# First attention of a hybrid block: outputs kept by channel and divided by GpSimd, maxima turned by VectorE

## The chip, the core and the metric

The kernel runs on one core of a Trainium2 chip. The metric is the device time of one execution in microseconds (us), here the median of three runs. A profile holds one execution. In it PE is TensorE (the matrix engine), PEld its weight loads, DVE VectorE, ACT ScalarE, POOL GpSimd, and SPq the queue of SyncE, which issues nearly all DMAs of this kernel. Each engine works through its own list of instructions in order, and engines wait for each other by semaphores.

## What is computed

A block of four layers on x of 1024 tokens x 512 channels, all in fp32: attention A (32 heads of 16 channels, causal, rotary), a mixture-of-experts layer, attention B (32 heads of 128 channels), and the same mixture again. The change concerns attention A alone:

```python
xq, xk = rotary(x @ wq.T), rotary(x @ wk.T)          # 32 heads of 16
scores = einsum("bqhd,bkhd->bhqk", xq, xk) * hd**-0.5
scores = where(causal, scores, -1e30)
probs  = softmax(scores)                              # max, exp, divide by the sum
out    = einsum("bhqk,bkhd->bqhd", probs, xv).reshape(B, T, C)
x      = x + out @ wo.T
```

## The kernel before

Attention A takes its heads in eight groups of four (index c, 0 to 7). A head has 16 channels and is padded to 32 partitions, so four heads fill 128. Channel 16 of a head in `qT` holds the negated row maximum, and in `kT` it is 1: one matmul then gives score minus maximum. Column 16 of `v_p` is 1, so that row 16 of an output is the sum of the exponentials.

Two passes run side by side, one group apart. The row pass of group c+1 (`row_scores`, L325) makes scores with queries on partitions, and VectorE takes their maxima (`maxima`: L342 for a first part, L345 for the rest). `with_maxima` turns the maxima from partitions to a row and puts them into `qT`. The column pass of group c (`col_scores`, L378) makes the scores again with keys on partitions, ScalarE takes exp (L397), and `product` (L417) multiplies with the values into one PSUM bank `outs[c, qc]`, for each half qc of the queries. When that is complete, ScalarE copies it (L426), and `normalize` divides.

`step(rc, cc, n)` is one of nine pieces of both passes, done in two half steps of two heads each. A half step has scores for two row tiles and two column tiles, then the maxima, the exponentials, what is due in the list `later`, and half of a product that is two pieces behind. `later` holds functions with a count of how many calls of `due` they wait. All score tiles, and everything else that goes through PSUM here, rotate through the seven banks of the pool `ps_s`; a tile has to be read by VectorE or ScalarE before its bank is written again. The output bank `ps_o` is a single one. For c below 7, the outputs of qc=1 are complete in piece 8 of their own group and those of qc=0 in piece 1 of the next group.

The order on each engine is made by a scheduler from the order of the program, so an instruction may stand ahead of where the program calls it; TensorE's order around the change is scores, half a product, scores, half a product.

In `normalize` (L430) TensorE turns the output back to tokens on partitions (four transposes, tile `tp_o`), ScalarE copies it (L437), VectorE inverts the sums (L439) and GpSimd multiplies (L441). `tail` and `projected` then turn every token tile again to channels on partitions (`gather`: four transposes, tile `tp_ao`, and a copy by VectorE, L1043) and multiply with `wo` (`out_projection`, L1049). The first two token tiles are done right after the attention, the other six inside the loop of the first mixture layer, each with a layer norm, its transposes (`tp_f`) and the router's matmuls (`pr_f`, L568).

Of the kernel before, what the change touches and what calls it, by code (L numbers as in the profile page):

```python
# [9 lines left out]
F32 = mybir.dt.float32  # L10
BF16 = mybir.dt.bfloat16
AF = mybir.ActivationFunctionType
ALU = mybir.AluOpType
# [3 lines left out]
P = 128  # L17
T = 1024
NT = T // P
C = 512  # L20
# [44 lines left out]
class Block:  # L65
# [174 lines left out]
    def attend_a(self, ctx_pool, pt, work, ps_s, ps_o, qT, kT, v_p, project_qk, project_v, midway, tail):  # L240
        nc, tc = self.nc, self.tc
        HC = P // PADA
        with ExitStack() as ctx:
            cp = ctx.enter_context(tc.tile_pool(name="a_c", bufs=1))
            qk = ctx.enter_context(tc.tile_pool(name="a_qk", bufs=2))
            o_sb = []

            next(project_qk)

# [44 lines left out]
            def neg(c, half):  # L294

                if (c, half) not in negs:
                    negs[c, half] = qk.tile([P, HC, NT // 2], F32, tag="neg", name=f"neg{c}_{half}", bufs=3)
                return negs[c, half]
# [56 lines left out]

            def with_maxima(c, half):

                rows = HC * NT // 2
                ps = ps_s.tile([P, QC], F32, tag="s", name=f"tp_m{c}{half}")[:rows, :P]
                nc.tensor.transpose(ps, neg(c, half).rearrange("p h i -> p (h i)"), self.ident)  # L360
                t = qk.tile([P, P], F32, tag="negT", name=f"negT{c}_{half}")[:rows, :]
                nc.scalar.copy(t, ps)
                for j in range(HC):
                    row = j * PADA + DA
                    nc.sync.dma_start(
                        qT[row : row + 1, c, half * QC : (half + 1) * QC].rearrange("o (i t) -> o i t", t=P),
                        t[j * NT // 2 : (j + 1) * NT // 2, :],
                    )

            def col_scores(c, n, heads, made):  # L370

# [27 lines left out]
            def product(c, n, p):  # L399

                pieces = col_pieces(c, n)
                middle = pieces[-1][-1] // 2
                steps = by_cols(c)
                for lo, hi in ((0, middle), (middle, 2 * middle)):
                    for qc, b, x0, _, at, end in pieces:
                        p0, p1 = max(lo, at), min(hi, end)
                        if p0 >= p1:
                            continue
                        first = (c, qc) not in outs
                        if first:  # L410
                            outs[c, qc] = ps_o.tile([P, QC], F32, tag="o", name=f"oT{c}_{qc}")
                        last = p1 == end and b == [x[1] for y in steps for x in y if x[0] == qc][-1] and all(
                            x[0] != qc for y in steps[n + 1 :] for x in y
                        )
                        o = outs[c, qc]
                        for j in range(HC):
                            nc.tensor.matmul(  # L417
                                o[rows_of(j), x0 + p0 - at : x0 + p1 - at],
                                lhsT=v_cols(b, c * HC + j),
                                rhs=p[:, j, p0:p1],  # L420
                                start=first,
                                stop=last,
                            )
                        if last:
                            oT = work.tile([P, QC], F32, tag="w", name=f"oTs{c}_{qc}")
                            nc.scalar.copy(oT, o)  # L426
                            later.append([0, lambda qc=qc, oT=oT: normalize(c, qc, oT)])
                    yield

            def normalize(c, qc, oT):  # L430
                if not o_sb:
                    o = ctx_pool.tile([P, NT, C], F32, tag="o", name="o")
                    o_sb.extend(o[:, i] for i in range(NT))
                ps = self.transpose4(ps_s, [oT[:, i * P : (i + 1) * P] for i in range(4)], f"o{c}{qc}", tag="s")
                pv = ps.rearrange("p a (h d) -> p a h d", d=PADA)
                os = qk.tile([P, 4, HC, DA + 1], F32, tag="os", name=f"os{c}_{qc}")
                nc.scalar.copy(os, pv[:, :, :, : DA + 1])  # L437
                rs = qk.tile([P, 4, HC], F32, tag="rs", name=f"rsa{c}_{qc}")
                nc.vector.reciprocal(rs, os[:, :, :, DA])  # L439
                for a in range(4):  # L440
                    nc.gpsimd.tensor_tensor(  # L441
                        o_sb[qc * 4 + a][:, c * HC * DA : (c + 1) * HC * DA].rearrange("p (h d) -> p h d", d=DA),
                        os[:, a, :, :DA],
                        rs[:, a, :].unsqueeze(2).to_broadcast([P, HC, DA]),
                        ALU.mult,
                    )

            def drain(gens):
                gens = list(gens)
# [10 lines left out]
            def due():  # L460

                for x in list(later):
                    x[0] -= 1
                    if x[0] < 0:
                        later.remove(x)
                        x[1]()

            def step(rc, cc, n):
# [8 lines left out]
                for half in range(2 if both else 1):  # L477
# [11 lines left out]
                    if cc is not None:  # L489
                        exponentials(cc, n, cols, madeT, p)  # L490
                    due()
                    next(turns, None)
                drain([turns])
                if rc is not None:

                    for half in range(2):
                        if n == max(m for m, y in enumerate(by_rows(rc)) for x in y if x[0] // 4 == half):
                            later.append([0, lambda half=half: with_maxima(rc, half)])


            for i in range(1, NT):
# [13 lines left out]
            for item in pending:  # L515
                due()
                drain([product(*item)])
            tail(o_sb, ps_s, work, later)
        return o_sb

# [490 lines left out]
def hybrid_block_kernel(  # L1013
# [23 lines left out]
    ao = ctx.enter_context(tc.tile_pool(name="a_out", bufs=1))  # L1037
    wo = ao.tile([P, KC, C], F32, tag="wo", name="a_wo")

    def gather(o, i, work, tp, wtag, tag):  # L1040
        ps = blk.transpose4(tp, [o[i][:, k * P : (k + 1) * P] for k in range(KC)], f"ao{i}", tag)
        oT = work.tile([P, KC * P], F32, tag=wtag, name=f"aoT{i}").rearrange("p (k t) -> p k t", t=P)
        nc.vector.tensor_copy(oT, ps)  # L1043
        return oT

    def out_projection(i, oT, ps_m, tag):
        pm = ps_m.tile([P, C], F32, tag=tag, name=f"pm_ao{i}")
        for kc in range(KC):
            nc.tensor.matmul(pm, lhsT=oT[:, kc, :], rhs=wo[:, kc, :], start=(kc == 0), stop=(kc == KC - 1))  # L1049
        nc.vector.tensor_add(blk.x[i], blk.x[i], pm)  # L1050

    def tail(o, ps, work, later):
        oTs = [gather(o, i, work, ps, "w", "s") for i in range(2)]
        out_projection(0, oTs[0], ps, "s")
        while later:
            later.pop(0)[1]()
        out_projection(1, oTs[1], ps, "s")

    weights = [w_baseT, w_rhT, lora_B, b_base]
    f_ctx = ExitStack()  # L1060
# [8 lines left out]
    def projected(work, tp, ps_m):  # L1069
        yield  # L1070
        yield
        oT = gather(o, 2, work, tp, "oT", "tp")
        for i in range(2, NT):
            nxt = gather(o, i + 1, work, tp, "oT", "tp") if i + 1 < NT else None
            out_projection(i, oT, ps_m, "pm")
            oT = nxt
            yield

    xnT, xn = [], []
# [85 lines left out]
```

## Time and profile before

| | us |
|---|---|
| median of 3 runs | 1640.02 (1639.93 to 1641.65) |
| the profiled execution | 1641.65 |
| its span, first to last instruction | 1639.6 |
| TensorE busy in it | 1621.2 |
| VectorE, ScalarE, GpSimd busy | 1099.2, 551.5, 350.8 |
| from the first column scores to the end of the last product of attention A | 119.95 to 387.1 |
| from there to the end of the last output projection | 387.1 to 428.0 |

Busy time is a share of the span by engine. Groups of instructions are listed by line, engine, operation and tile with their mean duration; a line of the timeline has start, duration, engine, line, operation, the tiles written and read, and in square brackets the idle time before it and what ended it. Transposes by TensorE all have line L99, so they are told apart by their tiles.

### The profile page before, as it was taken

Reading aid. Unit: us, or ns where it says so; the run is one execution under the profiler, and the core shown is the slowest. Engines: PE = TensorE matmul, PEld = TensorE weight load, DVE = VectorE, ACT = ScalarE, POOL = GpSimd, SP = SyncE. Lnnn points to the kernel's source line nnn. Section 1 sums busy time; section 2 is a strip of 40 time slices with the busy share of each in tenths; the row PEclk is TensorE's granted clock in tenths of the full one; section 3 lists DMA queues with packets and bytes.
Section 4 is the critical chain, followed back from the end, with each engine's and each line's share of the span. In section 5 each row is a group of like instructions: output and inputs, shape, how many; then the busy total and the mean of one; then the engine's idle time right before and its main releaser. Section 6 shows DMA issues by size and latency. Waiting matters only on the chain.

```text
span 1639.6 us, 32629 instructions
## 1 busy us (share of the span) xinstructions
PE 1621.2 (99%) x13320; PEld 955.1 (58%) x13320; DVE 1099.2 (67%) x2832; ACT 551.5 (34%) x1202; POOL 350.8 (21%) x524
## 2 busy tenths in 40 slices
PE   9999999999999999999999999999999999999989
PEld 5545555555565667566655665756665566556654
DVE  4557777762635876867777677676767767777762
ACT  2316565664222332233233223223323322322230
POOL 3000000002222323123223212222322221221140
PEclk9999999999999999999999999999999999999999
DMA  5000000001012201200200210120020011000001
GB/s 199 1 1 2 2 2 3 2 3 40 1 53 66 62 2 43 49 27 26 65 27 26 47 46 1 40 52 27 27 65 27 27 43 56 1 27 27 2 1 51
DMA packets 60870, 52.08 MB, mean 32 GB/s; under 512 B 5745, under 2 KB 47473, under 8 KB 60721
## 3 DMA queue, kind: packets, MB, share of 16 engines
q1 hardware_dynamic: 59408, 46.06, 9.8%
q0 software_dynamic: 784, 2.90, 0.5%
q8 instruction: 104, 1.70, 0.4%
q10 hardware_dynamic: 528, 1.05, 0.2%
q14 instruction: 46, 0.37, 0.1%
HBM read 30.98 MB, written 2.10 MB: 20 GB/s over the span
## 4 chain that ended last, share of the span: by engine, by line
PE 73%; DVE 3%; POOL 1%; ACT 1%; issue 0%; ACTq 0%; DVEq 0%
PE s L825 15%; PE pq L779 14%; PE o L869 13%; PE wo L676 13%; PE kv L734 7%; PE pm_f L633 3%; PE or L869 3%; PE pm_ao L1049 1%; PE st L805 1%; PE pm_f L634 1%; PE tp_k L99 0%; DVE p L827 0%; PE pr_f L568 0%; PE oT L417 0%; POOL x L559 0%; DVE pT L852 0%
## 5 line engine op out<-in xcount | busy, mean ns | idle before, releaser
L834 ACT ACTIVATE p<-p,nm 128x1024 f32<-128x1024 f32 (+7 forms) x256 | 198.1, 774 | 405.8 <-DVE nm L832 363.3
L837 POOL TENSOR_SCALAR p<-p,rs 128x1024 f32<-128x1024 f32 (+7 forms) x256 | 190.3, 745 | 645.7 <-DVE rs L836 621.8
L825 PE MATMUL s<-kT,qT 128*128 128x512 f32 (+3 forms) x768 | 296.0, 493 | 1.9 <-DVE p L827 1.8
L852 DVE STREAM_TRANSPOSE pT<-p 128x640 f32<-128x640 f32 (+4 forms) x256 | 169.0, 670 | 127.5 <-PE o L869 83.8
L779 PE MATMUL pq<-xnTb,wq 128*128 128x512 f32 x512 | 243.0, 597 | 0.0
L676 PE MATMUL wo<-wo,oT 128*128 128x512 f32 x512 | 240.7, 593 | 1.8 <-DVE nm L832 1.8
L827 DVE SCALAR_TENSOR_TENSOR p<-s,rq,rel 128x512 f32<-128x512 f32 (+3 forms) x384 | 224.0, 601 | 24.6 <-PE s L825 23.4
L825 PEld LDWEIGHTS s<-kT,qT 128*128 128x128 f32 x768 | 140.8, 190 | 164.8 <-issue 117.2
L869 PEld LDWEIGHTS o<-pT,va 32*128 32x128 f32 x5248 | 210.7, 185 | 25.5 <-issue 17.9
L869 PE MATMUL o<-pT,va 32*128 32x256 f32 (+5 forms) x5248 | 220.0, 321 | 0.0
L831 DVE TENSOR_REDUCE nm<-p 128x1 f32<-128x1024 f32 (+7 forms) x256 | 188.8, 738 | 2.9
L397 ACT ACTIVATE p<-sT 128x512 f32<-128x512 f32 (+1 forms) x292 | 155.7, 592 | 97.7 <-PE s L325 46.2
L325 PE MATMUL s<-kT,qT 32*128 32x512 f32 (+3 forms) x768 | 164.1, 520 | 0.0
L378 PE MATMUL sT<-qT,kT 32*128 32x128 f32 (+3 forms) x1152 | 155.4, 401 | 0.2 <-DMA qT<-negT 0.2
L676 PEld LDWEIGHTS wo<-wo,oT 128*128 128x128 f32 x512 | 94.6, 190 | 89.0 <-issue 76.3
L779 PEld LDWEIGHTS pq<-xnTb,wq 128*128 128x128 f32 x512 | 92.4, 190 | 88.8 <-issue 79.7
L734 PE MATMUL kv<-wkv,xnTb 128*128 128x256 f32 x512 | 116.5, 380 | 0.8 <-DVE qT L789 0.5
L378 PEld LDWEIGHTS sT<-qT,kT 32*128 32x128 f32 x1152 | 80.9, 184 | 50.8 <-issue 24.6
L734 PEld LDWEIGHTS kv<-wkv,xnTb 128*128 128x128 f32 x512 | 96.2, 190 | 20.0 <-issue 4.0
L342 DVE TENSOR_REDUCE part<-s 128x1 f32<-128x512 f32 x128 | 81.9, 686 | 36.3 <-PE s L325 32.3
L417 PE MATMUL oT<-p,v_p 128*32 128x128 f32 (+1 forms) x1552 | 89.8, 332 | 0.0
L441 POOL TENSOR_TENSOR o<-os,rsa 128x64 f32<-128x64 f32 x64 | 16.7, 292 | 323.5 <-DVE rsa L439 308.5
(154 smaller groups left out, 1617.6 us busy)
## 6 DMA issues: line engine op xcount, KB each, us to landing
va<-v SPq DMA_DIRECT2D x256, 64.0 KB
wq<-in_b_WqT_dram SPq DMA_DIRECT2D x8, 1024.0 KB
wo<-in_b_WoT_dram SPq DMA_DIRECT2D x8, 1024.0 KB
x<-in_x_dram SPq DMA_DIRECT2D x8, 256.0 KB
wkv<-in_b_WkT_dram SPq DMA_DIRECT2D x8, 256.0 KB
wkv<-in_b_WvT_dram SPq DMA_DIRECT2D x8, 256.0 KB
out_dram<-x SPq DMA_DIRECT2D x8, 256.0 KB
wq<-in_a_wqT_dram ACTq DMA_DIRECT2D x1, 1024.0 KB
```

Source lines behind the costliest of these rows:

```text
L325: nc.tensor.matmul(made[j][:, at:end], lhsT=qT[rows_of(j), c, i * P : (i + 1) * P], rhs=kT[rows_of(j), c, kc * QC : kc * QC + end - at], s ...
L378: nc.tensor.matmul(made[j][:, at:end], lhsT=kT[rows_of(j), c, b * P : (b + 1) * P], rhs=qT[rows_of(j), c, qc * QC + x0 : qc * QC + x1], st ...
L676: nc.tensor.matmul(ps, lhsT=oTs[g, h][:, t * P : (t + 1) * P], rhs=wo[:, h, :], start=(h == heads[0]), stop=(h == heads[-1]))
L734: nc.tensor.matmul(ps.rearrange("p a b -> p (a b)"), lhsT=xnT[:, kc, i * P : (i + 1) * P], rhs=wkv[:, kc].rearrange("p a b -> p (a b)"), s ...
L779: nc.tensor.matmul(ps, lhsT=wq[:, kc, hh * DB : (hh + 1) * DB], rhs=xnT[:, kc, cols], start=(kc == 0), stop=(kc == KC - 1))
L825: nc.tensor.matmul(s, lhsT=qT[:, i * P : (i + 1) * P], rhs=kT[:, lo:hi], start=True, stop=True)
L827: nc.vector.scalar_tensor_tensor(p[:, lo:hi], s, rq[:, i : i + 1], rel[:, at + lo : at + hi], ALU.mult, ALU.add)
L831: nc.vector.tensor_reduce(nm, p[:, :w], AX.X, ALU.max, negate=True)
L834: nc.scalar.activation(p[:, :w], p[:, :w], AF.Exp, bias=nm, scale=slope, accum_out=ss)
L837: nc.gpsimd.tensor_scalar(p[:, :w], p[:, :w], rs, 1.0, ALU.mult, ALU.mult)
L852: nc.vector.transpose(PT[:, i : i + (NT - 1) * (m - 1) + 1 : NT - 1, :], p[:, : m * P].rearrange("p (j k) -> p j k", k=P))
L869: nc.tensor.matmul(cols(o[:, a], j), lhsT=vs[g][rows, j * NB + b, :], rhs=moving(j, rows, slice(b * B, (b + 1) * B)), start=(j == js[0] an ...
```

## The change

Outputs of attention A stay with channels on partitions. `normalize` is called as soon as the output bank is copied. It issues five DMAs: one that spreads the four rows of sums over 128 partitions of 16 numbers (`sums`), and four that put each head's 16 channels into the tile that the output projection will read (`to`). Two functions go into `later`: `invert` (VectorE inverts the sums; one DMA brings them back to four rows of `over`, and another spreads each of these over 16 partitions) and `multiply` (GpSimd multiplies 64 partitions x 512 in place). The transposes of `normalize` and `gather` and the copies behind them are gone, and the output projections read `outs_sb` directly.

`with_maxima` is called at the end of the step, not one `due` later. VectorE turns the 128x16 maxima in 32x32 blocks, the 16 columns written twice to fill a block; four DMAs then write, each one block of 32 query positions of all four heads, 16 pieces of 128 bytes. Before, TensorE and ScalarE made the turn and there was one DMA per head, four pieces of 512 bytes.

Where a step has only one of the two passes, `due` is called twice.

```diff
             def with_maxima(c, half):
-                rows = HC * NT // 2
-                ps = ps_s.tile([P, QC], F32, tag="s", name=f"tp_m{c}{half}")[:rows, :P]
-                nc.tensor.transpose(ps, neg(c, half).rearrange("p h i -> p (h i)"), self.ident)
-                t = qk.tile([P, P], F32, tag="negT", name=f"negT{c}_{half}")[:rows, :]
-                nc.scalar.copy(t, ps)
-                for j in range(HC):
-                    row = j * PADA + DA
-                    nc.sync.dma_start(
-                        qT[row : row + 1, c, half * QC : (half + 1) * QC].rearrange("o (i t) -> o i t", t=P),
-                        t[j * NT // 2 : (j + 1) * NT // 2, :],
-                    )
+                t = qk.tile([P, B], F32, tag="negT", name=f"negT{c}_{half}")
+                twice = neg(c, half).rearrange("p h i -> p (h i)").unsqueeze(1).to_broadcast([P, 2, B // 2])
+                nc.vector.transpose(t.rearrange("p (a m) -> p a m", a=2), twice)
+                to = qT[:, c, half * QC : (half + 1) * QC].rearrange("(j r) (i a t) -> j r a i t", r=PADA, a=P // B, t=B)
+                for a in range(P // B):
+                    m = a * B
+                    nc.sync.dma_start(to[:, DA, a], t[m : m + B // 2, :])
...
                         if last:
-                            oT = work.tile([P, QC], F32, tag="w", name=f"oTs{c}_{qc}")
+                            oT = qk.tile([P, QC], F32, tag="oT", name=f"oTs{c}_{qc}")
                             nc.scalar.copy(oT, o)
-                            later.append([0, lambda qc=qc, oT=oT: normalize(c, qc, oT)])
+                            normalize(c, qc, oT)
...
             def normalize(c, qc, oT):
-                if not o_sb:
-                    o = ctx_pool.tile([P, NT, C], F32, tag="o", name="o")
-                    o_sb.extend(o[:, i] for i in range(NT))
-                ps = self.transpose4(ps_s, [oT[:, i * P : (i + 1) * P] for i in range(4)], f"o{c}{qc}", tag="s")
-                pv = ps.rearrange("p a (h d) -> p a h d", d=PADA)
-                os = qk.tile([P, 4, HC, DA + 1], F32, tag="os", name=f"os{c}_{qc}")
-                nc.scalar.copy(os, pv[:, :, :, : DA + 1])
-                rs = qk.tile([P, 4, HC], F32, tag="rs", name=f"rsa{c}_{qc}")
-                nc.vector.reciprocal(rs, os[:, :, :, DA])
-                for a in range(4):
-                    nc.gpsimd.tensor_tensor(
-                        o_sb[qc * 4 + a][:, c * HC * DA : (c + 1) * HC * DA].rearrange("p (h d) -> p h d", d=DA),
-                        os[:, a, :, :DA],
-                        rs[:, a, :].unsqueeze(2).to_broadcast([P, HC, DA]),
-                        ALU.mult,
-                    )
+                if not outs_sb:
+                    outs_sb.append(ctx_pool.tile([P, KC, T], F32, tag="o", name="o"))
+                at = c % 2 * HC * DA
+                to = outs_sb[0][at : at + HC * DA, c // 2, qc * QC : (qc + 1) * QC]
+                sums = qk.tile([P, QC // B], F32, tag="sums", name=f"sums{c}_{qc}")
+                over = qk.tile([P, QC], F32, tag="over", name=f"over{c}_{qc}")
+                row = P // 2 - at
+                by_head = oT.rearrange("(j r) t -> j r t", r=PADA)
+                nc.sync.dma_start(sums, by_head[:, DA, :].rearrange("j (x e) -> j x e", x=B))
+                for j in range(HC):
+                    nc.sync.dma_start(to[j * DA : (j + 1) * DA, :], by_head[j, :DA, :])
+                def invert():
+                    nc.vector.reciprocal(sums, sums)
+                    inverses = over[row : row + HC, :]
+                    nc.sync.dma_start(inverses.rearrange("j (x e) -> j x e", x=B), sums)
+                    nc.sync.dma_start(over[at : at + HC * DA, :], inverses.unsqueeze(1).to_broadcast([HC, DA, QC]))
+                def multiply():
+                    nc.gpsimd.tensor_tensor(to, to, over[at : at + HC * DA, :], ALU.mult)
+                later.append([3, invert])
+                later.append([8, multiply])
...
                     due()
+                    if not both:
+                        due()
...
-                            later.append([0, lambda half=half: with_maxima(rc, half)])
+                            with_maxima(rc, half)
...
-    def gather(o, i, work, tp, wtag, tag):
-        ps = blk.transpose4(tp, [o[i][:, k * P : (k + 1) * P] for k in range(KC)], f"ao{i}", tag)
-        oT = work.tile([P, KC * P], F32, tag=wtag, name=f"aoT{i}").rearrange("p (k t) -> p k t", t=P)
-        nc.vector.tensor_copy(oT, ps)
-        return oT
-
-    def out_projection(i, oT, ps_m, tag):
+    def out_projection(oT, i, ps_m, tag):
...
-            nc.tensor.matmul(pm, lhsT=oT[:, kc, :], rhs=wo[:, kc, :], start=(kc == 0), stop=(kc == KC - 1))
+            nc.tensor.matmul(pm, lhsT=oT[:, kc, i * P : (i + 1) * P], rhs=wo[:, kc, :], start=(kc == 0), stop=(kc == KC - 1))
...
-    def tail(o, ps, work, later):
-        oTs = [gather(o, i, work, ps, "w", "s") for i in range(2)]
-        out_projection(0, oTs[0], ps, "s")
+    def tail(oT, ps, later):
+        out_projection(oT, 0, ps, "s")
         while later:
             later.pop(0)[1]()
-        out_projection(1, oTs[1], ps, "s")
+        out_projection(oT, 1, ps, "s")
...
     def projected(work, tp, ps_m):
         yield
         yield
-        oT = gather(o, 2, work, tp, "oT", "tp")
         for i in range(2, NT):
-            nxt = gather(o, i + 1, work, tp, "oT", "tp") if i + 1 < NT else None
-            out_projection(i, oT, ps_m, "pm")
-            oT = nxt
+            out_projection(o, i, ps_m, "pm")
             yield
```

## The prediction

> **What bounds the kernel now.** I read the busy table first, then the busy time by stretches of attention A, then the timeline around the outputs of one group.
>
> ```profile
> PE 1621.2 (99%) x13320; PEld 955.1 (58%) x13320; DVE 1099.2 (67%) x2832; ACT 551.5 (34%) x1202; POOL 350.8 (21%) x524
> ```
>
> ```profile
> 150.00:361.00 211.00, 211.00 (x2732) 108.36 (x2730) 156.03 (x501) 129.93 (x257) 12.53 (x48) 1.00 0.01 3
> 361.00:387.00 26.00, 24.15 (x425) 13.72 (x425) 1.03 (x7) 20.26 (x45) 3.13 (x12) 1.00 0.01 2
> ```
>
> A stretch shows its window, its length, then busy us of TensorE, its weight loads, VectorE, ScalarE and GpSimd, the clock, the DMA share and GB/s. TensorE never idles from 150 to 361, so each instruction taken from it there is worth its time, if nothing else begins to hold it. VectorE has 55 us to spare of 211; GpSimd and the DMA engines are nearly empty. From 361 TensorE idles 1.85 us: 1.02 ahead of the turn of the outputs (6, qc=0) and 0.83 ahead of (7, 0), both waiting for ScalarE's copy of the single output bank.
>
> ```profile
> 184.88 0.60 ACT L426 COPY oTs<-oT 128x512 f32<-128x512 f32 x1
> 185.57 0.56 DVE L345 CUSTOM_DVE_ANT_0 junk<-s,mask 128x384 f32<-128x384 f32 x1 [0.20 <-PE sT L378]
> 185.62 0.66 PE L99 MATMUL tp_o<-ident,oTs 128*128 128x128 f32 x4
> 186.21 0.64 PE L417 MATMUL oT<-p,v_p 128*32 128x256 f32 x8
> 186.95 0.25 DVE L439 RECIPROCAL rsa<-os 128x16 f32<-128x16 f32 x1
> ...
> 194.19 0.59 ACT L426 COPY oTs<-oT 128x512 f32<-128x512 f32 x1
> 194.92 0.66 PE L99 MATMUL tp_o<-ident,oTs 128*128 128x128 f32 x4
> 194.99 1.29 DVE L342 TENSOR_REDUCE part<-s 128x1 f32<-128x512 f32 x2 [0.44 <-PE s L325]
> 195.51 0.64 PE L417 MATMUL oT<-p,v_p 128*32 128x256 f32 x8
> ```
>
> These are group 1's two halves: the copy, the four turns (0.59 from start to start: 185.62 to 186.21, 194.92 to 195.51), and right beside the copy VectorE's maxima, which free the score banks that TensorE writes next. The inversion at 186.95 stands behind the second half's maxima of piece 8.
>
> ```profile
> 116.96 2.57 SPq L365 DMA_DIRECT2D qT<-negT  x4
> 119.95 0.69 PE L378 MATMUL sT<-qT,kT 32*128 32x512 f32 x1 [0.24 <-DMA qT<-negT]
> ```
>
> This is the only measure of a small transfer between partitions that something waits for: the third of the four is issued at 118.29 and TensorE starts at 119.95, 1.66 later.
>
> **The change part by part.** (1) *Turns of the outputs.* Sixteen groups of four leave TensorE, 0.59 each. For (6,0) and (7,0) the wait for the copy stays with whatever follows, as the output bank is still one; the turn alone goes.
>
> (2) *Turns of the maxima.* Sixteen, 0.20 each by the starts (187.85 to 188.06). VectorE's 32x32 turn isn't in this stage; its 128x128 turns elsewhere take 0.30, so about 0.2, inside its 55 us. ScalarE loses a copy. Still four DMAs, but of 16 pieces of 128 bytes; they may land as late as before, or up to 0.35 later (2.0 against 1.65). The column pass that reads them is some half steps on, so I take 0; without that cover it is 0.35 per half. The first group's goes one turn and copy earlier: the 0.24 idle at 119.95 goes.
>
> (3) *The inversion.* This is the part that speaks against the change. `invert` waits three calls, but the scheduler's order for the changed kernel puts it on VectorE's queue directly behind the first half's maxima of piece 8 for (c,1), and behind the first tile's maxima of piece 2 for (c,0), c = 0 to 5. By the times of before these places come 0.12 us before the copy ends, and about 0.9 after. The inversion now waits for the DMA `sums`, which starts when the copy ends. VectorE works in order, so the remaining maxima of that piece stand behind it, their score banks stay full, and TensorE's next scores, which reuse them seven tiles on, wait.
>
> Let L be the time from the issue of `sums` to its landing. From below it is 1.65, the wait above, whose DMAs have one 512-byte piece on each of four engines. The nearest case with many pieces, the values' load into the padded tile (128 pieces over 16 engines), completes 2.0 after issue. The row says 1.65 to 2.0. The Trainium skill, "DMA: Bandwidth & Descriptors", section "Why a DMA increments its semaphore by 16 and not by 1", speaks against: the number of engines is the largest up to 16 that divides the slowest dimension of both sides. Here the source's is 4, so four engines take 32 pieces of 64 bytes each, in series. No run here shows the 64-byte case; small packets occupy an engine 7 to 9 ns (4 bytes) and 13 (128 bytes), so with 10 to 20 each, 1.65 + 31 x 0.010 to 0.020 = 2.0 to 2.3. I take 2.1 and keep 1.65 to 2.5.
>
> For (c,1): maxima that began at 185.57 start at 185.48 + L + 0.25. Set against what TensorE has queued in banks already free, and with the turn out of its way, this leaves a stall of L - 0.57, less 0.1 for the score tile that runs ahead: 1.4. For (c,0), placed a piece later, L - 1.4, less 0.1: 0.6. A group thus gains 2 x (0.59 + 0.20) = 1.58 and loses 2.0: +0.4 for each of c = 0 to 5, +2.5 together. With L = 1.65, the row's lower end, the loss is 0.98 + 0.15 and a group gains 0.45 net: 5.2 less in all than by the rule's 2.1. The stall returns in each group, since the turns don't build a lead for TensorE that VectorE can take back.
>
> For (6,1) the inversion still waits, but with few maxima behind it: 0.58 and 0.20 gained, 0.2 lost, -0.6. (6,0), (7,0): -0.58 each, -1.2. The two maxima's turns of group 0 and what remains of group 7's: -0.6. The first idle: -0.24.
>
> (4) *Copies of heads.* Five more DMAs on SP's queue in each half; nothing waits for the four `to` before the multiply. With a pitch of 0.665 each (measured on the maxima's), 3.3 us of issue per half, against 13 us between halves. The maxima's DMAs and the inverses' (two) queue behind them; for (c,1), SP issues `sums`, four `to`, four of the maxima, inverses, broadcast: 11 x 0.665 = 7.3 us, while the next column pass reads the second half's maxima only at its own pieces, so I price it at nothing; without that cover, the five in front cost up to 3.3 per group. If the maxima's are the late ones, scores of the column pass wait, by DMA.
>
> (5) *Multiply.* GpSimd gives up four 0.29 multiplies and takes one of 64x512. Its nearest row, 128x512, is 1.27; it is idle 94% of this stretch: nothing.
>
> (6) *The end of attention and f1's front.*
>
> ```profile
> 387.08 1.09 PE L99 MATMUL tp_ao<-ident,o 128*128 128x128 f32 x8
> ...
> 388.52 3.70 PE L1049 MATMUL pm_ao<-a_wo,aoT 128*128 128x512 f32 x8 [0.35 <-DVE aoT L1043]
> ...
> 404.05 3.60 PE L1049 MATMUL pm_ao<-a_wo,aoT 128*128 128x512 f32 x8
> ```
>
> Eight groups of turns, 0.435 each by the starts (408.85 to 409.29), 3.5. The last output turn, 0.43; the idle before the projection, 0.35, before the next tile's, 0.28. The copy of `aoT` (0.69) no longer stands between a turn and VectorE's add: where TensorE idled 0.87 at 396.1 before the router's turn, I leave about 1.2, since VectorE's last inversion stands ahead of the first token tile's add and waits for `sums` (7,1), from 387 to about 389.5. Sum: 3.5 + 0.43 + 0.35 + 0.28 + 0.7 - 0.35 = 4.9; 40.9 us become 36.0. Hidden here: the last half's broadcast, queued behind the 1 MB load of attention B's weights on SP (moving until about 395.5), and its multiply, behind GpSimd's work for token tiles 0 and 1. The multiply ends an estimated 14 us after attention's end; tile 2's projection, at once behind the first two, needs only the halves of qc=0, and those of qc=1 serve tile 4 on. If it is late, tile 4 waits.
>
> Sum: +2.5 - 0.6 - 1.2 - 0.6 - 0.24 - 4.9 = -5.0. Span 1634.6, against 1639.6. The profiled execution took 1641.65, 1.63 above the median shown, with 2.05 outside the span; so it would be 1636.6, and the median 1640.02 - 5.0 = 1635.0.
>
> **The rivals.** *The stalls hide.* If TensorE had enough tiles ahead to ride over VectorE's waits, attention would keep 6 x 1.58 = 9.5 more plus the 2.5: about 12 below, 1623. For: VectorE idles 55 us of 211. Against: a tile is reused after seven, and in a half step four are new.
>
> *The sums land late* (the other side). Place: VectorE's inversion in piece 8 and piece 2 of six groups. Each further us of L costs 12 x 1 us, two stalls in six groups. It breaks even with before at L = 2.5 and is slower by over 0.2% from 2.8; at 3.0, 1635.0 + 0.9 x 12 = 1646. For: 64-byte pieces on few engines, and other DMAs between. Against: the values' load, 128 pieces, took 2.0.
>
> *The last division becomes the bound of the mixture's start.* Five DMAs, an inversion, two DMAs behind weight loads: if the multiply comes 5 us later than I put it, the 4.9 of the end are lost: 1640.
>
> *The change doesn't do what it says*, the inversion being placed so that even the gain is taken back exactly: about 1640.
>
> **How the numbers follow.** Chances: mine (L from 1.75 to 2.5) 0.50, with its own range of 1630 to 1640; hidden stalls 0.08; late sums 0.30, spread over 1644 to 1655; late division 0.08; nothing 0.04. A measurement of this kernel tells 0.2% (3.3 us) from no change, so faster means below 1636.7 and slower above 1643.3. Faster: two thirds of mine (L below 2.24), 0.33, and 0.08: 0.41. Slower: 0.30. Same: the other third, 0.17, and 0.12: 0.29. The range leaves out the hidden stalls' 0.08 and the upper 0.12 of late sums, from L = 3.2: 1628 to 1648.
>
> **What would show it.** The transposes `tp_o`, `tp_m` and `tp_ao` gone from TensorE; VectorE's inversion with idle time before it, released by the DMA of `sums`, about 2.3 us for (c,1) and 1.3 for (c,0), some 24 us in all; TensorE no longer full from 150 to 361, about 1.4 idle near each group's piece 8 and 0.6 near piece 2, ended by VectorE's maxima; the end's 40.9 at 36. The prediction is wrong if `sums` lands outside 1.65 to 2.5, if TensorE idles for the maxima's DMAs instead, or if tile 4's projection waits for GpSimd's product.

## The result, and the profile after

The changed kernel takes 1668.16 us (median of four, 1666.55 to 1670.84) against 1639.97 of before: 1.017 times as long, 95% interval 1.0157 to 1.0182, 28 us slower. The forecast was 1635.0 in a range of 1628 to 1648. Of the cases it named, the late sums came true (given 0.30), past the 1655 that it put as their upper end, and so did the late last division (given 0.08), at token tile 0 and not at tile 4, where it was looked for.

The profiled execution took 1668.17 with a span of 1666.3. First the busy table and the two stretches of attention A, of the changed kernel.

```profile
PE 1631.4 (98%) x13208; PEld 951.2 (57%) x13208; DVE 1094.8 (66%) x2840; ACT 546.1 (33%) x1170; POOL 355.6 (21%) x476
```

```profile
150.00:361.00 211.00, 200.90 (x2344) 96.14 (x2344) 138.83 (x461) 111.99 (x206) 13.88 (x11) 0.94 0.11 17
361.00:387.00 26.00, 26.00 (x372) 14.22 (x364) 16.44 (x52) 14.09 (x27) 1.27 (x1) 0.93 0.07 10
```

TensorE has fewer instructions and is busy 10 us longer. That is the first sign: it not only waits, it runs slower. The granted clock was 1.00 in the first stretch before, and is 0.94 now.

One place explains most of it. This is the timeline of the changed kernel at the outputs (5, qc=0), where the forecast had a stall of 0.6:

```profile
352.27 0.59 ACT L422 COPY oTs<-oT 128x512 f32<-128x512 f32 x1
352.89 0.56 SPq L438 DMA_DIRECT2D sums<-oTs  x1
353.50 3.98 SPq L440 DMA_DIRECT2D o<-oTs  x4
357.72 0.25 DVE L443 RECIPROCAL sums<-sums 128x16 f32<-128x16 f32 x1 [3.83 <-DMA sums<-oTs]
357.89 2.42 DVE L342 TENSOR_REDUCE part<-s 128x1 f32<-128x512 f32 x4
358.57 1.22 PE L374 MATMUL sT<-qT,kT 32*128 32x512 f32 x1 [2.02 <-DVE part L342]
```

The sums are issued 0.03 us after the copy ends and the inversion starts 4.83 later. VectorE idles 3.83 with four maxima behind it, and TensorE idles 2.02 until the first of them has read its bank. Then its matmuls of 512 columns take 1.22 where they took 0.69. The same moments in slices of 1 us (columns as before; the clock is the third from the right) say why:

```profile
356.00:357.00 1.00, 0.55 (x4) 0.00 (x0) 0.00 (x0) 0.36 (x1) 0.13 (x1) 1.00 0.38 75
357.00:358.00 1.00, 0.00 (x0) 0.00 (x0) 0.28 (x2) 0.24 (x1) 1.00 (x1) 0.88 0.18 41
358.00:359.00 1.00, 0.43 (x2) 0.43 (x4) 1.00 (x2) 0.00 (x0) 0.13 (x1) 0.50 0.14 33
...
363.00:364.00 1.00, 1.00 (x8) 0.20 (x8) 0.26 (x1) 0.30 (x1) 0.00 (x0) 0.50 0.24 25
...
365.00:366.00 1.00, 1.00 (x25) 0.71 (x18) 0.24 (x2) 0.00 (x0) 0.00 (x0) 1.00 0.22 23
```

From 357.75, within the idle, the granted clock is 0.50 for 6.8 us, and TensorE is busy in 6.0 of them. The same happens in each of the groups 0 to 5, once in a group: idles of 2.37, 1.17, 1.84, 1.15, 1.55 and 2.02, together 10.1 us, and half clocks of 3.4, 3.4, 6.8, 3.4, 3.4 and 6.8 us, together 27.3, of which 26.3 lie behind the idles.

At (c,1) the picture is the one that was forecast, smaller. Group 5 again:

```profile
342.63 0.59 ACT L422 COPY oTs<-oT 128x512 f32<-128x512 f32 x1
...
343.25 0.56 SPq L438 DMA_DIRECT2D sums<-oTs  x1
...
345.20 0.25 DVE L443 RECIPROCAL sums<-sums 128x16 f32<-128x16 f32 x1 [2.09 <-DMA sums<-oTs]
```

Here L, from the issue of `sums` to the start of the inversion, is 1.95 (1.87 to 1.96 for the seven groups 0 to 6), in the range that was given. At (c,0) it is 4.0 to 5.2. What differs is what stands ahead on the DMA engines. For group 0 SyncE issues the broadcast of (0,1) at 156.82 and the sums of (0,0) at 158.84. The transfers from 158 to 163.2 (the busy share of the 16 DMA engines in 40 slices, packets, and the queues):

```profile
DMA  1223121141131402312114623140231131402311
...
DMA packets 66, 0.14 MB, mean 28 GB/s; under 512 B 3, under 2 KB 3, under 8 KB 65
## 3 DMA queue, kind: packets, MB, share of 16 engines
q1 hardware_dynamic: 65, 0.13, 22.6%
```

In 5.2 us little moves but the broadcast's 64 pieces of 2 KB, on 3.6 engines of 16 (22.6%), about 300 ns a piece. The 128 pieces of 64 bytes of the sums, 9 to 11 ns each, run from 163.19 on, behind it. Where they have the engines for themselves, all 128 take 0.33 us.

The end went the other way too. TensorE's first output projection and what it waits for:

```profile
400.84 0.56 SPq L438 DMA_DIRECT2D sums<-oTs  x1
...
407.51 0.25 DVE L443 RECIPROCAL sums<-sums 128x16 f32<-128x16 f32 x1 [9.61 <-DMA sums<-oTs]
...
408.94 2.84 PE L1052 MATMUL pm_ao<-a_wo,o 128*128 128x512 f32 x6
...
410.03 0.61 SPq L446 DMA_DIRECT2D over<-over  x1
...
417.30 1.26 POOL L449 TENSOR_TENSOR o<-o,over 64x512 f32<-64x512 f32 x1 [8.66 <-DMA o<-oTs]
...
418.62 6.53 PE L1052 MATMUL pm_ao<-a_wo,o 128*128 128x512 f32 x10 [6.83 <-POOL o L449]
```

Token tile 0 already needs the product of (7, qc=0), and that is late. Its copy ends at 397.70, but its sums are issued 3.14 later, because SyncE's queue held (6,0)'s DMAs that waited for each other. They land behind (6,0)'s broadcast after 6.7, its own broadcast takes until 417, and TensorE idles 6.83. The clock is at half from 415.8 to 422.6, so for 4.0 us behind the idle.

The sum, from the two profiles: the first column scores start 1.0 earlier; from there to the last product it is 290.1 us instead of 267.2 (+22.9); from there to the last output projection 45.1 instead of 41.0 (+4.1). That is +26.0 of the span's +26.7.

### The profile page after: what moved, and what is told of

It is laid out like the page before. It is cut to its first block, busy times and chain, and to the rows that moved or that the text cites. A ratio compares the mean times of both kernels' runs of the same rounds, so it can differ in the third digit from the quotient of the medians.

```text
span 1666.3 us, 32497 instructions
## 1 busy us (share of the span) xinstructions
PE 1631.4 (98%) x13208; PEld 951.2 (57%) x13208; DVE 1094.8 (66%) x2840; ACT 546.1 (33%) x1170; POOL 355.6 (21%) x476
## 4 chain that ended last, share of the span: by engine, by line
PE 92%; DVE 3%; DMA 2%; ACT 1%; POOL 1%; issue 1%; SPq 0%; ACTq 0%; DVEq 0%; POOLq 0%
PE s L834 15%; PE pq L788 13%; PE o L878 13%; PE wo L685 12%; PE sT L374 7%; PE kv L743 6%; PE oT L413 4%; PE pm_f L642 3%; PE or L878 3%; PE s L325 2%; PE pj_v L185 2%; PE pj_q L185 2%; PE pj_k L185 2%; DMA sums<-oTs 2%; PE pm_ao L1052 1%; PE st L814 1%
## 5 line engine op out<-in xcount | busy, mean ns | idle before, releaser
L374 PE MATMUL sT<-qT,kT 32*128 32x128 f32 (+3 forms) x1152 | 176.8, 414 | 10.1 <-DVE part L342 10.1
L325 PE MATMUL s<-kT,qT 32*128 32x512 f32 (+3 forms) x768 | 180.3, 539 | 0.0
L374 PEld LDWEIGHTS sT<-qT,kT 32*128 32x128 f32 x1152 | 86.2, 188 | 71.1 <-issue 26.1
L413 PE MATMUL oT<-p,v_p 128*32 128x128 f32 (+1 forms) x1552 | 93.7, 344 | 1.8 <-ACT oTs L422 1.8
L449 POOL TENSOR_TENSOR o<-o,over 64x512 f32<-64x512 f32 x16 | 20.3, 1266 | 345.6 <-DMA o<-oTs 227.4
```

The source lines that it names most:

```text
L325: nc.tensor.matmul(made[j][:, at:end], lhsT=qT[rows_of(j), c, i * P : (i + 1) * P], rhs=kT[rows_of(j), c, kc * QC : kc * QC + end - at], s ...
L374: nc.tensor.matmul(made[j][:, at:end], lhsT=kT[rows_of(j), c, b * P : (b + 1) * P], rhs=qT[rows_of(j), c, qc * QC + x0 : qc * QC + x1], st ...
```

## The experiments

Each kernel was timed beside the kernel before on the same chip (medians of 1640.7 to 1641.3; beside the changed kernel 1639.97). "Attention" is the time in the profile from the first column scores to the last product, before 267.2; "end" is from there to the last output projection, before 41.0.

| kernel | median us | ratio to before, 95% | attention | end | TensorE idle ahead of tile 0's projection |
|---|---|---|---|---|---|
| the changed kernel | 1668.16 | 1.0157 to 1.0182 | 290.1 | 45.1 | 6.83 |
| `e1_bcast4` | 1651.56 | 1.0054 to 1.0084 | 274.5 | 43.4 | 4.57 |
| `e2_pinned` | 1640.38 | 0.9989 to 1.0007 | 259.8 | 47.9 | 9.28 |
| `e3_gpinv` | 1642.53 | 1.0003 to 1.0021 | 256.7 | 53.4 | 14.52 |
| `e4_maxima` | 1638.30 | 0.9978 to 0.9991 | 263.8 | 41.0 | (transposed as before) |
| `e5_sums_act` | 1671.21 | 1.0175 to 1.0205 | 292.8 | 45.2 | 7.29 |
| `e6_pinned_bcast4` | 1634.41 | 0.9944 to 0.9974 | 256.1 | 44.7 | 6.67 |
| `e7_half` | 1647.99 | 1.0024 to 1.0054 | 262.3 | 51.8 | 14.02 |
| `e8_poolq` | 1636.11 | 0.9968 to 0.9986 | 256.3 | 48.9 | 9.85 |
| `e9_poolq_end` | 1634.21 | 0.9948 to 0.9971 | 256.3 | 45.3 | 7.02 |
| `e10_half0` | 1678.68 | 1.0220 to 1.0250 | 302.6 | 44.9 | 7.16 |
| `e11_split` | 1629.99 | 0.9914 to 0.9944 | 257.8 | 37.6 | 1.32 |
| `e12_quarter` | 1630.73 | 0.9920 to 0.9953 | 263.0 | 36.0 | none |

**Take VectorE out of it.** The inversion moves to GpSimd, all DMAs stay:

```diff
-                    nc.vector.reciprocal(sums, sums)
+                    nc.gpsimd.tensor_tensor(sums, sums, minus1, ALU.pow)
```

> The inversion of the sums moves from VectorE to GpSimd (a power of -1 there); all DMAs stay as they are. Theory (VectorE's wait in its queue is what holds TensorE): sums of (c, 0) are still late by 4 to 5 us, but VectorE idles for none of them, TensorE is full from 125 to the last group's outputs, the clock stays whole in attention A: of 1668.2 the waits and half clocks go, 6 x 5.4 = 32, so about 1636, with the end's idle of 6.8 us still there. Rival (the eleven DMAs of a half hold the column pass through late maxima): TensorE still idles, now ended by the DMA into qT, and the time is over 1650.

Two stretches of that kernel, with the columns of before, and its end:

```profile
150.00:361.00 211.00, 209.47 (x2824) 108.88 (x2828) 154.99 (x499) 130.42 (x245) 52.74 (x25) 1.00 0.13 20
```

```profile
391.46 1.26 POOL L451 TENSOR_TENSOR o<-o,over 64x512 f32<-64x512 f32 x1 [9.33 <-DMA o<-oTs]
392.77 3.78 PE L1054 MATMUL pm_ao<-a_wo,o 128*128 128x512 f32 x4 [14.52 <-DMA o<-oTs]
392.80 2.90 POOL L445 TENSOR_TENSOR sums<-sums,minus 128x16 f32<-128x16 f32 x1
```

The clock is 1.00 again, and what is left of idle in the stretch, 1.5 us, lies behind 355.8, at (6,0): 1.02 for ScalarE's copy of the output bank, and then this:

```profile
358.40 1.14 PE L376 MATMUL sT<-qT,kT 32*128 32x512 f32 x8 [0.50 <-DMA qT<-negT]
```

Attention falls from 290.1 to 256.7: all of the loss there, 33.4 us, hangs on VectorE's place in its queue, and the full gain of the turns, 10.5, appears. The rival (late maxima) falls for the groups 0 to 5: that 0.50 us, for the last group's maxima, is the only wait for `qT`. Their DMAs were issued at 354.88, 3.6 us behind VectorE's turn, since the inverses ahead of them on SyncE's queue waited for GpSimd until 354.1. The median came out 6 above the 1636 expected: GpSimd's power on 128x16 takes 2.89 us against VectorE's 0.25, and it stands in the chain at the end, which is 8.3 us longer than the changed kernel's, with 14.5 us idle and the clock at half for 17 us, 5 of them behind the idle.

**Leave VectorE the inversion, but in its place in the program,** three half steps later:

```diff
-                    nc.vector.reciprocal(sums, sums)
+                    tc.keep_in_program_order(nc.vector.reciprocal(sums, sums))
```

> The changed kernel with the inversion held in its place in the program on VectorE (three half steps after the output's copy, behind the maxima of those half steps); all DMAs and the engine stay. Theory (only the early place of the inversion in VectorE's queue holds TensorE): as with the inversion on GpSimd, no TensorE idle of over 0.3 us between 125 and the last group, no half clock there, the first column scores to the last product in about 257 us (before 267, the changed kernel 290); the idle ahead of the first output projection stays between 5 and 15 us: 1632 to 1644. Rival (the division's DMAs cost TensorE time of their own, whatever VectorE does): over 265 us for that stretch, and over 1650.

As expected: attention 259.8, no half clock in it, 1640.38. One idle of 0.50 appeared at 336.2. So it is the place that costs and not the engine. The 3.1 us above the kernel with GpSimd's power stay open; with four broadcasts they are gone (`e6_pinned_bcast4`, 256.1).

**One of the two places each.** VectorE inverts (c,1) alone, then (c,0) alone, with `if not qc:` in the line below; GpSimd has the rest:

```diff
+                    if qc:
                         nc.vector.reciprocal(sums, sums)
+                    else:
+                        nc.gpsimd.tensor_tensor(sums, sums, minus1, ALU.pow)
```

> VectorE inverts the sums of (c, 1) alone, GpSimd those of (c, 0): what the wait at (c, 1) costs by itself. From the drift of TensorE's instructions in the changed kernel, 0.9 to 1.0 us at each of six (c, 1), with no idle of TensorE over 0.3 shown and no half clock: against the kernel with both on GpSimd (1642.5), 6 more in attention A, 1647 to 1650. The prediction's own figure was 1.4 each, 8.4: 1651. If the wait at (c, 1) is hidden: 1642 to 1644.

> The complement of the kernel in which VectorE inverts (c, 1) alone: here it inverts (c, 0) alone, GpSimd the rest. In the changed kernel each (c, 0) holds TensorE for 1.15 to 2.4 us of idle and another 0.5 to 1, and its clock is at half for 3.4 or 6.8 us after: about 4.5 for each of six. Against the kernel with all on GpSimd (1642.5): 1642.5 + 27 = 1665 to 1672, with five or six stretches of half clock in attention A. If the waits at both places are needed for the loss: below 1655.

(c,1) alone adds 5.6 to attention, 0.93 for each of six, with no idle shown and no half clock: the wait stands in records that count as busy, as TensorE's stretch shows all 211.00 us filled. The 1647.99 fit, and the forecast's 1.4 was too high. (c,0) alone was underestimated: expected were 27, and it adds 46 us, 7.7 each, with idles of 3.8 to 4.1 and 6.8 us of half clock in each group. Here is its stretch:

```profile
150.00:361.00 211.00, 191.24 (x2282) 91.93 (x2279) 133.91 (x439) 106.78 (x198) 30.01 (x16) 0.92 0.11 16
```

The two don't add up: 5.6 and 46 against 33.4 together. In the second kernel the (c,1) inverses come later (GpSimd's 2.9 us), so their broadcast is issued only 0.66 ahead of the (c,0) sums (280.53 and 281.19), which then land after 6.5 to 6.8 instead of 4.0 to 5.2. The closer the sums follow the broadcast, the later they land: in the changed kernel they follow it by 2.0 to 3.3.

**What makes the sums of (c,0) late?** Three kernels ask. The broadcast as four DMAs:

```diff
-                    nc.sync.dma_start(over[at : at + HC * DA, :], inverses.unsqueeze(1).to_broadcast([HC, DA, QC]))
+                    for j in range(HC):
+                        nc.sync.dma_start(
+                            over[at + j * DA : at + (j + 1) * DA, :],
+                            inverses[j : j + 1, :].unsqueeze(1).to_broadcast([1, DA, QC]),
+                        )
```

> The one DMA that spreads four rows of inverses over 64 partitions becomes four, one for each head (16 pieces of 2 KB each). In the changed kernel that one DMA occupies four DMA engines for 5.3 us (158.04 to 163.4) and the sums of (c, 0), issued at 158.84, land only after it. Theory (the broadcast ahead on the queue makes the sums late, VectorE waits for them, TensorE idles, and its clock then falls to half): the sums of (c, 0) land in 2.0 to 2.5 us instead of 4.0 to 5.2, the TensorE idles of 1.15 to 2.4 us near (c, 0) shrink below 0.6, no half clock in attention A, and the idle of 6.8 us ahead of the first output projection is down to 0 to 3; 1668.2 - 6 x 4.5 - 5 = about 1636 (1630 to 1645). Rival (64-byte pieces on four engines are late by themselves): the sums of (c, 0) still land 4 us or more after issue, and the time stays above 1660.

The direction was right, the size was not: L at (c,0) is 3.3 to 3.9, idles of 0.45 to 1.31, one half clock of 3.4 us in attention, 1651.56. All 16 engines now take part, but the 64 pieces still need 4.9 us (193.4 to 198.3 in group 1; the last starts at 197.6) instead of 5.3. The transfers from 193.4 to 197.8:

```profile
DMA  9766731600099959603909960906660699909400
...
q1 hardware_dynamic: 118, 0.14, 76.3%
```

76% of 16 engines are busy for 0.14 MB. The first 16 pieces take 518 ns each, the other 48, which overlap with them and with each other, 920.

The sums from another queue, ScalarE's:

```diff
-                nc.sync.dma_start(sums, by_head[:, DA, :].rearrange("j (x e) -> j x e", x=B))
+                nc.scalar.dma_start(sums, by_head[:, DA, :].rearrange("j (x e) -> j x e", x=B))
```

> The changed kernel with the DMA of the sums issued by ScalarE, right behind its own copy, instead of by SyncE; all else as it is. If the sums wait because they stand behind the broadcast in one queue, they land in 2 to 3 us and the time falls to about 1640 to 1648. If they wait because the same four DMA engines are busy, whichever queue they come from, they still land after 4 us or more and the time stays at 1660 to 1670.

L at (c,0) is 4.1 to 5.4, the time 1671.21. Another queue doesn't help; the transfers share the engines.

The broadcast cut to a quarter of its bytes:

```diff
-                    nc.sync.dma_start(over[at : at + HC * DA, :], inverses.unsqueeze(1).to_broadcast([HC, DA, QC]))
+                    nc.sync.dma_start(over[at : at + HC * DA, :P], inverses[:, :P].unsqueeze(1).to_broadcast([HC, DA, P]))
...
-                    nc.gpsimd.tensor_tensor(to, to, over[at : at + HC * DA, :], ALU.mult)
+                    quarter = over[at : at + HC * DA, :P].unsqueeze(1).to_broadcast([HC * DA, QC // P, P])
+                    nc.gpsimd.tensor_tensor(four, four, quarter, ALU.mult)
```

> The changed kernel with the broadcast cut to a quarter of its bytes (128 of 512 columns in the same 64 rows; GpSimd multiplies all four quarters by the first one's inverses, so the outputs of attention A are not the reference's). VectorE still inverts early. If the broadcast ahead of the sums of (c, 0) is what makes them late, they land in 2.0 to 2.8 us (4.0 to 5.2 in the changed kernel), and TensorE loses at (c, 0) what the prediction said for an L of 2.1, 0.6 each, with no idle over 0.3 shown and no half clock; with 0.93 at each (c, 1): attention A in about 257 + 6 x 1.5 = 266 us, the time 1640 to 1646. If the sums are still late by 3.5 us or more, it was not the broadcast.

Its stretch, group 1's (c,0), and its first output projections:

```profile
150.00:361.00 211.00, 211.00 (x2724) 108.08 (x2728) 155.47 (x514) 126.50 (x234) 15.19 (x12) 1.00 0.07 13
```

```profile
193.06 0.59 ACT L422 COPY oTs<-oT 128x512 f32<-128x512 f32 x1
...
193.68 0.56 SPq L438 DMA_DIRECT2D sums<-oTs  x1
...
195.63 0.25 DVE L443 RECIPROCAL sums<-sums 128x16 f32<-128x16 f32 x1 [0.95 <-DMA sums<-oTs]
...
382.32 7.13 PE L1054 MATMUL pm_ao<-a_wo,o 128*128 128x512 f32 x16
```

VectorE still inverts early, and everything else is as in the changed kernel, but that three quarters of the queries are divided by the wrong sums. The broadcast ahead, now 64 pieces of 512 bytes at mostly 74 ns each, has ended at 193.14, before the sums are issued. They land in 1.87 to 2.09 at (c,0), TensorE is full, the clock stays whole, and the projection starts without a wait. 1630.73, 9 below the lower end expected, 1640: I had expected attention in 266 and it took 263.0, and had not expected the end to come free as well. Of the 263.0, 256.7 is the kernel without any wait and 5.6 the six (c,1), so a (c,0) with L at 1.9 to 2.1 costs 0.1.

**The turn of the maxima alone,** in the kernel before:

```diff
-                ps = ps_s.tile([P, QC], F32, tag="s", name=f"tp_m{c}{half}")[:rows, :P]
-                nc.tensor.transpose(ps, neg(c, half).rearrange("p h i -> p (h i)"), self.ident)
...
+                nc.vector.transpose(t.rearrange("p (a m) -> p a m", a=2), twice)
+                for a in range(P // B):
...
```

> The kernel before with one part of the change alone: the maxima are turned by VectorE and put into qT by four DMAs of 16 pieces each; outputs, division and end as before. Theory: sixteen turns of 0.2 us leave TensorE and the first column scores start about 0.7 to 1.2 earlier, nothing waits: 1640.0 - 3.2 - 0.8 = about 1636. Rival (these DMAs land later than before and the column pass waits): the same as before or slower, 1640 to 1645.

Attention 3.4 shorter, start 0.36 earlier, the median 2.65 below before. The profile's span is 2.8 below, though attention's end is 3.8 earlier; the rest is given back later, and where stays open. The turn takes VectorE 0.21 us.

**A better end.** With the held inversion, what is left to lose is the chain ahead of tile 0. Both cures together:

```diff
-                    nc.vector.reciprocal(sums, sums)
+                    tc.keep_in_program_order(nc.vector.reciprocal(sums, sums))
...
+                    for j in range(HC):
+                        nc.sync.dma_start(
...
```

> The held inversion and the four DMAs in place of one, together. If the idle ahead of the first output projection comes from the chain of DMAs of the last groups (sums, inverses, a broadcast of 5.3 us, one behind the other on SyncE's queue), the shorter broadcast takes 2 to 5 us from each link: 1624 to 1632, faster than before. If that idle comes from something else at the end, the time stays with that of the held inversion alone.

1634.41: faster than before, but 6.67 us of idle remain. SyncE issues the sums of (7,0) 7.1 us after the copy, as (6,0)'s inverses and broadcasts stand ahead of them and wait. Then these went to GpSimd's queue, for all groups with one broadcast (the first diff), or for the last two with four (the second):

```diff
-                    nc.sync.dma_start(inverses.rearrange("j (x e) -> j x e", x=B), sums)
-                    nc.sync.dma_start(over[at : at + HC * DA, :], inverses.unsqueeze(1).to_broadcast([HC, DA, QC]))
+                    nc.gpsimd.dma_start(inverses.rearrange("j (x e) -> j x e", x=B), sums)
+                    nc.gpsimd.dma_start(over[at : at + HC * DA, :], inverses.unsqueeze(1).to_broadcast([HC, DA, QC]))
```

```diff
+                    q = nc.gpsimd if c >= NCA - 2 else nc.sync
-                    nc.sync.dma_start(inverses.rearrange("j (x e) -> j x e", x=B), sums)
+                    q.dma_start(inverses.rearrange("j (x e) -> j x e", x=B), sums)
...
```

> The held inversion, and the two DMAs behind it (inverses, one broadcast) issued by GpSimd instead of SyncE. If the idle ahead of the first output projection (6.67 us with four broadcasts, 9.28 with one) comes from sums that stand on SyncE's queue behind DMAs that wait (sums of (7, 0) issued 5.5 to 7.1 us after the copy), the sums go out with the copy again, that idle falls below 3 us and no half clock follows: 1624 to 1630. If a DMA issued by GpSimd takes longer to land by as much, the idle stays: 1634 to 1641.

> The held inversion and four broadcasts for every half; those of the groups 6 and 7 (with their inverses) issued by GpSimd, the rest by SyncE. Same question as with the single broadcast on GpSimd's queue, with shorter broadcasts and GpSimd's queue used only at the end: the idle ahead of the first output projection between 0 and 3 us, 1624 to 1630; if five issues by GpSimd in a row cost as much as the wait on SyncE's queue, 1632 to 1638.

Both missed the first branch: idles of 9.85 and 7.02. The sums now go out with the copy and are inverted by 366.5, but the wait had only moved. GpSimd's queue holds (6,0)'s product, which waits for its broadcast until 372.5 to 373.7, and (7,0)'s inverses stand behind it. So the two groups were put on different queues, group 6 on GpSimd's and group 7 on SyncE's:

```diff
+                    tc.keep_in_program_order(nc.vector.reciprocal(sums, sums))
+                    q = nc.gpsimd if c == NCA - 2 else nc.sync
-                    nc.sync.dma_start(inverses.rearrange("j (x e) -> j x e", x=B), sums)
+                    q.dma_start(inverses.rearrange("j (x e) -> j x e", x=B), sums)
...
```

> The held inversion and four broadcasts for every half; GpSimd issues the inverses and broadcasts of group 6 alone, SyncE all others. With group 6 off SyncE's queue and group 7 off GpSimd's, the inverses of (7, 0) stand behind no waiting DMA: inverses issued at 366 to 368 (before 374 to 375), product by GpSimd done by 376, ahead of the first output projection's need at 378. The idle of 7 us there goes, and the half clock behind it: 1634.3 - 7 - 3.4 = about 1624 (1622 to 1628). If the end is bound by something else, 1630 or more.

```profile
370.05 0.97 SPq L446 DMA_DIRECT2D over<-sums  x1
...
376.70 2.84 PE L1057 MATMUL pm_ao<-a_wo,o 128*128 128x512 f32 x6
...
379.54 1.26 POOL L454 TENSOR_TENSOR o<-o,over 64x512 f32<-64x512 f32 x1 [5.74 <-DMA wkv<-in_b_WkT_dram]
380.85 4.56 PE L1057 MATMUL pm_ao<-a_wo,o 128*128 128x512 f32 x10 [1.32 <-POOL o L454]
```

The idle is 1.32, no half clock follows, the end takes 37.6. The median is 1629.99 (1626.76 to 1630.72), above the 1622 to 1628 expected and 0.7% below before: the fastest of the kernels that compute all of it. The profile is of the execution of 1626.76, with a mean granted clock of 1.000; the other three have 0.998 to 0.999, so some half clock is in them that this profile can't place. The inverses went out at 370.05, not at 366 to 368: SyncE issues the four copies of heads ahead of them, from 366.12 to 369.80. And TensorE waited 1.58 us at 359.68 for `qT`, the maxima of the last group.

## Why the prediction was wrong

**Part (3), the inversion, failed first in one term: L at (c,0).** Its form was right: the place in VectorE's queue, the maxima behind it, the banks that TensorE waits for. L of 2.1 was right for (c,1), where it measured 1.87 to 1.96, by the row (1.65 to 2.0) rather than by the rule's 2.0 to 2.3. The 64-byte pieces on few engines were the wrong suspect. At (c,0) L was 4.0 to 5.2, because the broadcast of (c,1) was on the same DMA engines. Put into the forecast's own formulas, the measured L's make the loss 25.7 us instead of 12, and the time about 1649 (an estimate from the twelve L's). So of the 33 us by which the forecast missed, about 14 are this term, 9 are the end (+4.1 instead of -4.9), and the clock, below, makes most of the rest.

**Part (4) is where that stood.** It lists the inverses and the broadcast among eleven issues and prices them by SyncE's time of issue. It asked what waits behind them on SyncE's queue, and not how long the broadcast then holds the DMA engines, nor which transfer meets it there: the next half's sums, issued 2.0 to 3.3 us behind. The rule about the number of engines, weighed for the sums, applied just as well to the broadcast, whose source also has four rows: 64 pieces of 2 KB on four engines (3.6 in the trace) are 16 in series, and the measured 300 ns make 4.8 of the 5.3 us. Only the duration of a piece could not be had from before, where 2 KB took 84 ns. The late maxima that this part priced at nothing cost nothing in the changed kernel; in four others TensorE waited for them in the last group, for 0.17 to 0.51 us in three and 1.58 in `e11_split`.

**The stall's size at given L.** For L of 1.9 the forecast's formulas give 1.2 at (c,1) and 0.4 at (c,0). Measured: 0.93 and 0.1. A little of each was covered.

**The clock was not in the sum at all.** "Each further us of L costs 12 x 1 us" takes a stall for its own length. Of the 33.4 us, 5.6 are (c,1), if it costs here what it costs alone. The other 27.8 are 10.1 of idle shown, 13.1 of half clock (an estimate: half of the 26.3 us behind the idles), and 4.6 that the records don't show. So a stall cost 2.3 times its shown length, and more with the remainder. The Trainium skill, "TensorE: Matmul & The Clock Gate", section "Part 1: The HAM clock gate", says that the array runs at half rate after an idle window of about 3.4 us and at full rate after a busy one. The half clocks here last 3.41 us or twice that, as the windows would have it; but the idles before them were of 1.15 to 2.4 us, shorter than a window, and the measurement decides (the last section has the details).

**Parts (1) and (2)** hold within 15%: without waits the forecast's gains in attention are 9.5 for six groups, 0.8 for (6,1), 1.2 for (6,0) and (7,0) and 0.6 for the remaining turns, 12.1; the kernels without VectorE's wait gain 10.5 to 11.1. **Part (6)** holds in its size and failed in its cover: without a wait the end takes 36.0, the number forecast, in the kernel with a quarter of the broadcast. But it said that tile 2's projection "needs only the halves of qc=0", took those as done, and looked at (7,1) alone. Tile 0 needs them first, and (7,0)'s chain was not added up: sums, inverses and a broadcast of 5 us, behind another such chain.

## What to carry to other kernels

A small transfer that something waits for can be as late as a large transfer in front of it on its DMA engines: for each DMA that a change adds, work out not only its issue but how long its pieces occupy which engines, and which waited transfer is next. An instruction that waits for a DMA belongs, on an in-order engine, behind the work that others wait for; here moving one 0.25 us instruction by three half steps was worth 28 us. A short stall of TensorE can cost more than twice its length, since the clock may be at half for several us behind it.

## What was not expected of the hardware

- **Half clock after short idles, on a grid.** Idles of TensorE of 1.15 to 2.4 us were followed by 3.41 or 6.83 us at a clock of 0.50, in six of six groups. In each profile in which the clock changes in attention A, it does so only at points that lie whole multiples of 3.41 us apart (in the changed kernel it falls at 166.60, 204.15, 241.69, 282.65, 320.20 and 357.75). So the half clock may begin well behind the idle, in work that waits for nothing. In group 0 the idle ended at 164.93:

```profile
163.19:166.60 3.41, 1.67 (x16) 0.50 (x16) 2.52 (x6) 0.57 (x2) 1.26 (x1) 1.00 0.22 45
166.60:170.01 3.41, 3.41 (x26) 1.10 (x26) 1.95 (x4) 1.17 (x3) 0.00 (x0) 0.50 0.13 14
```

  In the changed kernel the stretch of this grid ahead of each drop held 1.15 to 1.74 us of idle. But the amount alone doesn't decide either: in other kernels 0.98 in one stretch was followed by half clock (sums on ScalarE's queue), 1.28 by none (four broadcasts, an idle of 1.31), and an idle of 1.58 in `e11_split` by none. What else counts stays open.
- **A row sent to many partitions is slow.** 16 pieces of 2 KB from 16 partitions took 0.39 us, 133 ns each, on 16 engines; 16 from one partition took 1.2 us, 518 ns each, on as many (both with four broadcasts). Four engines with one row each moved the 64 pieces in 5.3 us, 16 engines in 4.9. That the single source partition is the limit is argued from this pair, not shown by itself.
- **GpSimd's power** on 128x16 took 2.89 us where its multiply of 64x512 took 1.26.
